# A graph-attention layer that gathers one row per row: own-column rows are gathered again, one table block fewer, x asked for in five requests

## The chip, the core and the metric

The kernel runs on one core of a Trainium2 chip. A core has five engines that run side by side, each with its own stream of instructions: TensorE (PE, matrix products), VectorE (DVE), ScalarE (ACT), GpSimd (POOL) and SyncE (SP, which only asks for transfers). Sixteen transfer engines move data between HBM and the core's memory (SBUF); SP and POOL put requests into queues of their own for them. The metric is the device time of one execution in microseconds. Three runs of the kernel before took 236.44, 237.49 and 237.79 us, median 237.49.

## What is computed

The reference is a graph-attention layer with a residual and a layer norm (4,096 nodes, 512 features, 4 heads):

```python
ht = (h @ W).reshape(N, N_HEADS, N_HIDDEN).transpose(1, 0, 2)
e = leaky_relu(src[:, :, None] + dst[:, None, :], 0.01) + adj_mat[None]
att = softmax(e, axis=-1)
h_prime = einsum('hij,hjd->hid', att, ht).mean(axis=0)
x = layernorm(x + h_prime)
```

adj (4,096 x 4,096, 67 MB) has, on its edges, weights that are uniform from 0.05 to 1e9, and 0 elsewhere; every node has an edge to itself. Against such numbers the scores from `src` and `dst` are tiny. So the softmax of a row is one-hot: all weight lies on the column of the row's largest adj. The kernel uses that: for each row it finds the column of the largest adj, gathers that row of x, multiplies it by the mean of the four heads' W, adds the row's own x and normalises. A test at the end shows whether the largest value led by enough in every row; where not, a general path (the function `general`) computes those blocks in full. With these inputs it is not entered.

## The kernel before, in words

The 4,096 rows are worked through as 32 blocks of 128 rows, one row to a partition. Block 0 is rows 0 to 127; blocks 1 to 31 interleave the others (partition p of block b holds row 128 + 31 p + b - 1). A block of adj is 2 MB; six buffers hold them.

The order of all work is written out by hand (`tc.manual_schedule()`): a loop over steps t = 0 to 31 (lines 536 to 597), and a tail after it (599 to 665). Each engine runs its instructions strictly in the order in which they are written. What happens to a block spreads over steps:

- In step t SP asks for adj of block t + 5 (`load_adj`). Before that, in the steps of the table `x_at` (line 530), it asks for blocks of x into `hold`. All these requests stand in one queue. The two requests for x of eight blocks each are 2 MB, the others in the table 1 MB.
- VectorE reduces adj of block t to maxima of short segments (`segment_maxima`, L208, two halves) and finds the segment that holds the row's maximum (`find_segment`, L215, L217). GpSimd turns that into a row number and fetches the segment itself (`fetch_segment`: `row` L224, `lead` L228).
- Two steps later VectorE finds the column within the segment (`find_column`, L270 and L276), in the steps of `END` (up to 19) behind the step's own `find_segment`, from step 20 on between the two halves of the reduction. GpSimd makes `col` of it (L278) and gathers the rows of x (`gather_rows`).
- At t = block + 3 TensorE turns the gathered rows (`turn`, L290; ScalarE copies the result, L292), adds the row's own x through a product with the identity (`residual`, L302) and multiplies by W (`products`, L309).
- From t = block + 4 on ScalarE takes sums and squares for the layer norm; every fourth step GpSimd makes scale factors of them (`rstd`, L379 to L383), and ScalarE finishes the block (L388) in `hold`, from where it is stored in the tail.

Three ways of gathering exist. In a plain block (0 and 24 to 31) GpSimd gathers all 128 rows (L253). In a block of `TABLED` (1 to 18) the rows whose column is below 128 are not gathered: ScalarE clears the tile one step after the block before (`fill_rows`, L239), GpSimd computes `away` (L245) and `there` (L259), which push such a row's number past the end of x, and gathers with a bounds check (L260), which leaves the cleared row as it is. What is missing is taken from a table of the 128 finished products (`spread`, `from_table`: L337, L339, L341, L349 and `low`, L267). In a block of `OWN` (19 to 23) the rows whose column is their own number are not gathered: ScalarE first copies the block's own x, which is in `hold`, into the tile (L239), and GpSimd computes `away` by comparing with `own` (L247).

GpSimd takes the work of a step in this order: up to step 19 `row`, `lead`, `start` of block t, then column and gather of block t - 2, then `rstd`; from step 20 on column and gather of block t - 2 first, then `row`, `lead`, `start` of block t, then `rstd`. Its requests go into one queue.

Of the kernel before, what the change touches and what calls it, by code (L numbers as in the profile page):

```python
# [9 lines left out]
F32 = mybir.dt.float32  # L10
BF16 = mybir.dt.bfloat16
U32 = mybir.dt.uint32
I32 = mybir.dt.int32
AF = mybir.ActivationFunctionType
OP = mybir.AluOpType
# [6 lines left out]
P = 128  # L22
# [4 lines left out]
EARLY = 18  # L27
LAST = 4
SKIP = 8192
TABLED = range(1, 19)  # L30
OWN = range(19, 24)


@with_exitstack
# [39 lines left out]
def leading_rows(ctx, tc, x, adj, W, a, out, ident, n_bad, any_bad):  # L74
# [8 lines left out]
    nc = tc.nc  # L83
    N, D = x.shape
    H = a.shape[0]
    KB, NB = D // P, N // P
    RB = NB - 1
    AHEAD = 5
    Q = 4
    PIECES = 4  # L90
    LATE = NB - Q
    BEHIND = LATE - Q
# [3 lines left out]
    hold = landing.tile([P, NB, D], F32, name="hold")  # L96
# [5 lines left out]
    once = ctx.enter_context(tc.tile_pool(name="once", bufs=1))  # L102
    small = ctx.enter_context(tc.tile_pool(name="small", bufs=5))
# [18 lines left out]
    def load_adj(ib):  # L122
        if 0 <= ib < NB:
            t = adj_t[ib] = adj_pool.tile([P, N], F32, name="adj_t")
            n = pieces(ib)
            for k in range(n):
                rows_of = adj_rows[ib - 1] if ib else adj[:P, :]
                nc.sync.dma_start(t[:, ts(k, N // n)], rows_of[:, ts(k, N // n)])

    def load_x(lo, n):  # L130
        if lo == 0:
            nc.sync.dma_start(hold[:, 0, :], x[:P, :])
            lo, n = 1, n - 1
        if n:
            nc.sync.dma_start(hold[:, ds(lo, n), :], x_rows[:, ds(lo - 1, n), :])
# [20 lines left out]
    for e, lo, hi in spans:  # L156
        if lo == 0:
            nc.gpsimd.iota(first[:, 0:1], pattern=[[0, 1]], base=0, channel_multiplier=N // e)
            lo = 1
        nc.gpsimd.iota(  # L160
            first[:, lo:hi], pattern=[[N // e, hi - lo]], base=(P + lo - 1) * N // e,
            channel_multiplier=RB * N // e,
# [7 lines left out]
    nc.gpsimd.memset(power, -0.5)  # L170
    eps = once.tile([P, 1], F32, name="eps")
    nc.gpsimd.memset(eps, EPS)
    numbers = once.tile([P, NB], I32, name="numbers")
    nc.gpsimd.iota(numbers, pattern=[[1, NB]], base=P - 1, channel_multiplier=RB)
    own = once.tile([P, NB], F32, name="own")
    nc.gpsimd.tensor_copy(own, numbers)
    zero = once.tile([P, 1], F32, name="zero")
    nc.gpsimd.memset(zero, 0.0)
    nth = once.tile([P, 1], I32, name="nth")
# [19 lines left out]
    low_of, pick_of = {}, {}  # L199

    def segment_maxima(ib, lo, hi):

        e = spans[span_of(ib)][0]
        if lo == 0:
            seg_of[ib] = small.tile([P, N // e], F32, name=f"seg{e}", bufs=2)
        n = max(pieces(ib), 2)
        for k in range(lo * n // PIECES, hi * n // PIECES):
            nc.vector.tensor_reduce(  # L208
                seg_of[ib][:, ts(k, N // e // n)],
                adj_t[ib][:, ts(k, N // n)].rearrange("p (s e) -> p s e", e=e), axis=AX.X, op=OP.max,  # L210
            )

    def find_segment(ib):
        seg = seg_of.pop(ib)
        nc.vector.max(out=top[:, ib, :], in_=seg)  # L215
        at = at_of[ib] = small.tile([P, 8], U32, name="at")
        nc.vector.max_index(at, top[:, ib, :], seg)  # L217
        if ib < NB - 1:
            fetch_segment(ib)
# [14 lines left out]
            start = at_of[ib] = small.tile([P, 1], U32, name="start")  # L234
            nc.gpsimd.tensor_tensor(start, at[:, 0:1], width[:, k : k + 1], op=OP.mult)

    def fill_rows(ib):
        y = y_t[ib] = y_pool.tile([P, D], F32, name="y")
        nc.scalar.copy(y, zero.to_broadcast([P, D]) if ib in TABLED else hold[:, ib, :])  # L239

    def skipped(ib, col):

        away = small.tile([P, 1], U32, name="away")
        if ib in TABLED:
            nc.gpsimd.tensor_scalar(away, col, float(P), float(SKIP), op0=OP.is_lt, op1=OP.mult)  # L245
        else:
            nc.gpsimd.tensor_scalar(away, col, own[:, ib : ib + 1], float(SKIP), op0=OP.is_equal, op1=OP.mult)  # L247
        return away

    def gather_rows(ib, col):  # L250
        if ib not in TABLED and ib not in OWN:
            y = y_t[ib] = y_pool.tile([P, D], F32, name="y")
            nc.gpsimd.indirect_dma_start(  # L253
                out=y, out_offset=None, in_=x,
                in_offset=bass.IndirectOffsetOnAxis(ap=col[:, :1], axis=0),
            )
            return
        there = small.tile([P, 1], U32, name="there")
        nc.gpsimd.tensor_tensor(there, col, skipped(ib, col), op=OP.add)  # L259
        nc.gpsimd.indirect_dma_start(  # L260
            out=y_t[ib], out_offset=None, in_=x,
            in_offset=bass.IndirectOffsetOnAxis(ap=there[:, :1], axis=0),
            bounds_check=N - 1, oob_is_err=False,
        )
        if ib in TABLED:
            low = low_of[ib] = small.tile([P, 1], BF16, name="low")
            nc.gpsimd.tensor_scalar(low, col, float(P), None, op0=OP.min)  # L267

    def find_inner(ib):
        nc.vector.max(out=inner[:, ib, :], in_=lead_of[ib])  # L270
# [1 line left out]
    def find_column(ib):  # L272
        if ib < BEHIND:
            find_inner(ib)
        within = small.tile([P, 8], U32, name="within")
        nc.vector.max_index(within, top[:, ib, :], lead_of[ib])  # L276
        col = small.tile([P, 1], U32, name="col")
        nc.gpsimd.tensor_tensor(col, at_of.pop(ib), within[:, 0:1], op=OP.add)  # L278
        gather_rows(ib, col)
# [71 lines left out]
    def row_norm(ib):  # L351
        sq = rows.tile([P, D], F32, name="sq")
        nc.scalar.activation(sq, hold[:, ib, :], AF.Square, accum_out=xx[:, ib : ib + 1])  # L353
# [24 lines left out]
    def rstd(i):  # L378
        nc.gpsimd.tensor_scalar(sd[:, i], sd[:, i], 1.0 / D, EPS, op0=OP.mult, op1=OP.add)  # L379
        nc.gpsimd.tensor_tensor(sd[:, i], sd[:, i], power[:, : i.stop - i.start], op=OP.pow)  # L380
        nc.gpsimd.tensor_mul(nm[:, i], nm[:, i], sd[:, i])
        if i.stop <= BEHIND:
            nc.gpsimd.tensor_scalar(sd[:, i], sd[:, i], -float(D), None, op0=OP.mult)  # L383
# [61 lines left out]
    def mean_of_heads(kb):  # L445
        o = psum.tile([P, D], F32, name="o")
        for h in range(H):
            nc.tensor.matmul(o, ident, hold[:, w_at + kb * H + h, :], start=(h == 0), stop=(h == H - 1))  # L448
        nc.scalar.activation(w_sum[:, kb, :], o, AF.Copy, scale=1.0 / H)  # L449
# [9 lines left out]
    def square_sums_of_a():  # L459
        sq = rows.tile([P, D], F32, name="sq")  # L460
        nc.scalar.activation(sq[: 2 * H, :], a_rows, AF.Square, accum_out=aa)
# [65 lines left out]
        nc.vector.tensor_reduce(total, pg, axis=AX.X, op=OP.add)  # L527
        nc.vector.tensor_scalar(any_bad, total, -1.0, float(N), op0=OP.mult, op1=OP.add)

    x_at = {Q - 1: (Q, 2 * Q), 3 * Q - 1: (3 * Q, Q), 4 * Q - 1: (4 * Q, 2 * Q)}  # L530
    squares = list(range(KB * H))
    squares_at = {t: 2 if t < 7 else 1 for t in range(3, 15)}
    COLUMN, PROJECT, STATS, FINISH = 2, 3, 4, 8
# [2 lines left out]
    for t in range(NB):  # L536
        if t == NB // 2:
            tc.mark_branch_hint_location("general", engines=HINTED)
        if t in x_at:
            load_x(*x_at[t])  # L540
        if t + AHEAD == NB - 1:
            load_x(LATE, Q)
        load_adj(t + AHEAD)
        middle = 1 if t == NB - 1 else 2
        segment_maxima(t, 0, middle)
        if t >= COLUMN and t not in END and t != COLUMN + 1:
            find_column(t - COLUMN)
        segment_maxima(t, middle, PIECES)
        if t == NB - 1:
            for ib in (BEHIND, BEHIND + 2):  # L550
                load_x(ib, 2)
        find_segment(t)
        if t in END:
            find_column(t - 1 if t <= COLUMN else t - COLUMN)
        if t + 1 in TABLED or t + 1 in OWN:
            fill_rows(t + 1)
        if t >= FINISH and t % Q == 0:
            rstd(slice(t - FINISH, t - FINISH + Q))
        if t < 2:
            mean_of_heads(t)  # L560
        elif t == 2:
            mean_of_heads(2)
            mean_of_heads(3)
            fill_table()
        if t == 0:
            square_sums_of_a()
        if t in (24, 26, 28):
            head_norms((t - 24) // 2)
        ib = t - PROJECT
        if t == NB - 1:  # L570
            for late in range(LATE, NB):
                row_norm(late)
        if t == NB - 2:
            residual(LATE)
            residual(LATE + 1)
        if ib >= 0:
            if ib in TABLED:
                spread(ib)
            turn(ib)
            if ib > BEHIND:  # L580
                products(ib - 1, KB - 1, KB)
            if ib < BEHIND:
                residual(ib)
            if ib in TABLED:
                from_table(ib)
            products(ib, 0, KB if ib < BEHIND else KB - 1)
            if ib == 0:
                split_table()
        for _ in range(squares_at.get(t, 0)):
            square_sum_of_w(squares.pop(0))  # L590
        if t >= BEHIND + STATS:
            put_by(t - STATS)
        elif t >= STATS:
            row_norm(t - STATS)
            parked_stats(t - STATS)
        if t > FINISH:
            finish(t - FINISH - 1)
# [248 lines left out]
```

## Time and profile before

| | |
|---|---|
| median of three runs (lowest, highest) | 237.49 us (236.44, 237.79) |
| profiled execution | 237.14 us |
| its span, first to last instruction | 235.6 us |
| busy: PE, DVE, ACT, POOL | 194.4, 190.9, 143.4, 117.0 us |
| moved | 96.31 MB, mean 409 GB/s |

The span is the profiled part of an execution; 1.54 us lie outside it. The digits of the page's lines are tenths of busy time in 40 slices of the span, 5.9 us each. In a line of the timeline stand the start, the duration, the engine, the line of the program, the operation, output<-input and, in brackets, how long the engine had been idle before and what ended that. A transfer's time to landing runs from its issue to the moment at which its data is there. A window's row ends with the clock that TensorE was granted (1.00 is full), the busy share of the transfer engines, and GB/s.

### The profile page before, as it was taken

How to read it: one execution, taken by the hardware profiler on the slowest of the kernel's cores; microseconds unless marked ns; L12 is line 12 of the kernel's file. 1: busy time of each engine (PE TensorE's matmuls, PEld its weight loads, DVE VectorE, ACT ScalarE, POOL GpSimd, SP SyncE). 2: the span in 40 equal slices, each digit the busy share in tenths (PEclk: the TensorE clock that was granted, in tenths of full speed). 3: DMA queues.
4: the chain of work that ended last, by engine and by line, in shares of the span. 5: the costliest groups of instructions: out<-in, count | busy, mean ns of one | idle time of the engine just before them, and what ended most of it. 6: DMA issues, size and time to landing. Idle time of an engine off the chain costs nothing.

```text
span 235.6 us, 2436 instructions
## 1 busy us (share of the span) xinstructions
PE 194.4 (83%) x573; PEld 92.9 (39%) x580; DVE 190.9 (81%) x301; ACT 143.4 (61%) x348; POOL 117.0 (50%) x275
## 2 busy tenths in 40 slices
PE   0069988778199929999899999999999969999890
PEld 0034443333144424455355444444444424444360
DVE  0538389799829999999999919996999999978782
ACT  3002213678077717899878878887756854399661
POOL 4020425615552775547764765673666447547300
PEclk9999999999679967999999999999999999999999
DMA  6999999999999999999999999999999999999954
GB/s 226 430 428 435 427 428 422 435 436 412 437 423 429 433 426 424 434 419 437 422 431 417 434 429 426 421 430 427 427 432 416 426 423 413 419 424 421 381 204 186
DMA packets 12546, 96.31 MB, mean 409 GB/s; under 512 B 2058, under 2 KB 2506, under 8 KB 7024
## 3 DMA queue, kind: packets, MB, share of 16 engines
q1 hardware_dynamic: 8928, 88.08, 88.5%
q0 software_dynamic: 3584, 8.02, 8.7%
q8 instruction: 5, 0.08, 0.1%
q14 instruction: 13, 0.11, 0.1%
q10 hardware_dynamic: 16, 0.02, 0.0%
HBM read 88.54 MB, written 8.39 MB: 411 GB/s over the span
## 4 chain that ended last, share of the span: by engine, by line
DMA 37%; PE 28%; DVE 10%; POOL 9%; issue 7%; ACT 6%; SPq 0%; POOLq 0%; DVEq 0%
DMA y<-in_x_dram,there 18%; PE o L309 16%; DMA adj_t<-in_adj_dram 14%; DVE seg L208 6%; DMA lead<-in_adj_dram,row 5%; PE o L302 4%; PE tp L290 4%; PE o L349 3%; POOL lead L228 3%; POOL sd L380 2%; PE o L397 2%; ACT yt L292 1%; ACT sq L457 1%; ACT sq L353 1%; DVE col L284 1%
## 5 line engine op out<-in xcount | busy, mean ns | idle before, releaser
L208 DVE TENSOR_REDUCE seg<-adj_t 128x128 f32<-128x2048 f32 (+3 forms) x66 | 144.0, 2209 | 29.1 <-DMA adj_t<-in_adj_dram 29.0
L309 PE MATMUL o<-w_sum,yt 128*128 128x512 f32 x248 | 113.4, 598 | 2.0 <-ACT yt L292 1.9
L309 PEld LDWEIGHTS o<-w_sum,yt 128*128 128x128 f32 x248 | 45.9, 191 | 53.8 <-issue 42.1
L292 ACT COPY yt<-tp 128x512 f32<-128x512 f32 x33 | 19.1, 578 | 33.7 <-PE tp L290 33.6
L228 POOL DMA_INDIRECT lead<-in_adj_dram,row x32 | 32.7, 1023 | 12.4 <-POOL row L224 12.4
L290 PE MATMUL tp<-ident,y 128*128 128x128 f32 x128 | 23.0, 304 | 17.9 <-DMA y<-in_x_dram,there 15.4
L260 POOL DMA_INDIRECT y<-in_x_dram,there x23 | 25.6, 1115 | 15.1 <-POOL there L259 6.8
L290 PEld LDWEIGHTS tp<-ident,y 128*128 128x128 f32 x128 | 18.7, 209 | 32.3 <-issue 30.8
L224 POOL TENSOR_TENSOR row<-at,first 128x1 uint32<-128x1 uint32 x32 | 6.1, 191 | 48.1 <-DVE at L217 43.7
L302 PE MATMUL o<-hold,ident 128*128 128x512 f32 x52 | 28.2, 629 | 0.0
L448 PE MATMUL o<-hold,ident 128*128 128x512 f32 x32 | 16.9, 694 | 13.7 <-DMA hold<-in_L_gnn_W_dram 13.7
L353 ACT ACTIVATE sq<-hold 128x512 f32<-128x512 f32 x32 | 19.9, 624 | 0.0
L388 ACT ACTIVATE hold<-hold,nm,sd 128x512 f32<-128x512 f32 x24 | 19.1, 802 | 0.0
L376 ACT ACTIVATE sq<-hold,nm 128x512 f32<-128x512 f32 x24 | 17.4, 724 | 0.8
L449 ACT ACTIVATE w_sum<-o 128x512 f32<-128x512 f32 x4 | 2.4, 597 | 22.7 <-PE o L448 22.7
L448 PEld LDWEIGHTS o<-hold,ident 128*128 128x128 f32 x32 | 7.1, 225 | 22.7 <-issue 22.2
L339 ACT ACTIVATE off<-px,minus 128x128 f32<-128x128 f32 x18 | 6.6, 368 | 13.9 <-PE px L337 13.9
L374 ACT ACTIVATE hold<-o 128x512 f32<-128x512 f32 x24 | 14.3, 597 | 0.8
L349 PE MATMUL o<-z,pick 128*128 128x512 bf16 x48 | 14.2, 399 | 0.4 <-ACT sq L353 0.2
L215 DVE MAX8 top<-seg 128x8 f32<-128x256 f32 (+2 forms) x32 | 11.6, 361 | 1.1
L217 DVE FIND_INDEX8 at<-top,seg 128x8 uint32<-128x256 f32 (+2 forms) x32 | 11.3, 352 | 0.0
L349 PEld LDWEIGHTS <-pick 128*128 128x128 bf16 x54 | 5.6, 104 | 14.0 <-issue 7.6
(117 smaller groups left out, 190.6 us busy)
## 6 DMA issues: line engine op xcount, KB each, us to landing
adj_t<-in_adj_dram SPq DMA_DIRECT2D x28, 2048.0 KB, 32.5
adj_t<-in_adj_dram SPq DMA_DIRECT2D x6, 1024.0 KB, 24.0
hold<-in_L_gnn_W_dram SPq DMA_DIRECT2D x2, 2048.0 KB, 16.5
hold<-in_x_dram SPq DMA_DIRECT2D x2, 2048.0 KB, 33.6
out_dram<-hold SPq DMA_DIRECT2D x7, 512.0 KB, 4.6
out_dram<-hold SPq DMA_DIRECT2D x3, 1024.0 KB, 13.2
hold<-in_x_dram SPq DMA_DIRECT2D x2, 1024.0 KB, 27.2
adj_t<-in_adj_dram SPq DMA_DIRECT2D x4, 512.0 KB, 19.9
```

Of the source, the lines that this page charges most:

```text
L208: nc.vector.tensor_reduce(seg_of[ib][:, ts(k, N // e // n)], adj_t[ib][:, ts(k, N // n)].rearrange("p (s e) -> p s e", e=e), axis=AX.X, op ...
L228: nc.gpsimd.indirect_dma_start(out=lead, out_offset=None, in_=adj_segs[e], in_offset=bass.IndirectOffsetOnAxis(ap=row[:, :1], axis=0),)
L260: nc.gpsimd.indirect_dma_start(out=y_t[ib], out_offset=None, in_=x, in_offset=bass.IndirectOffsetOnAxis(ap=there[:, :1], axis=0), bounds_c ...
L290: nc.tensor.transpose(tp[:, kb, :], y[:, ds(kb, P, KB)], ident)
L292: nc.scalar.copy(yt, tp)
L302: nc.tensor.matmul(o_ps[ib], ident, hold[:, ib, :], start=start, stop=False)
L309: nc.tensor.matmul(o_ps[ib], yt_of[ib][:, kb, :], w_sum[:, kb, :], start=(start and kb == 0), stop=(kb == KB - 1),)
L349: nc.tensor.matmul(o_ps[ib], pick, z[k], start=(start and k == 0), stop=False)
L353: nc.scalar.activation(sq, hold[:, ib, :], AF.Square, accum_out=xx[:, ib : ib + 1])
L376: nc.scalar.activation(sq, hold[:, ib, :], AF.Square, bias=nm[:, i], scale=-float(D), accum_out=sd[:, i])
L388: nc.scalar.activation(hold[:, ib, :], o, AF.Identity, bias=nm[:, i], scale=sd[:, i])
L448: nc.tensor.matmul(o, ident, hold[:, w_at + kb * H + h, :], start=(h == 0), stop=(h == H - 1))
```

## The change

`OWN` and all that serves it are gone (`own`, `numbers`, the copy of the block's own x, the comparison): blocks 19 to 23 are gathered whole, as plain blocks. Block 18 leaves `TABLED` and becomes a plain block too. `fill_rows` is now `clear_rows` and only clears. The table `x_at` becomes five requests for four blocks of x each, at steps 3 (blocks 4 to 7), 7 (8 to 11), 11 (12 to 15), 15 (16 to 19) and 18 (20 to 23), in place of blocks 4 to 11 at step 3, 12 to 15 at step 11 and 16 to 23 at step 15.

```diff
-TABLED = range(1, 19)
-OWN = range(19, 24)
+TABLED = range(1, 18)
...
-    numbers = once.tile([P, NB], I32, name="numbers")
-    nc.gpsimd.iota(numbers, pattern=[[1, NB]], base=P - 1, channel_multiplier=RB)
-    own = once.tile([P, NB], F32, name="own")
-    nc.gpsimd.tensor_copy(own, numbers)
...
-    def fill_rows(ib):
+    def clear_rows(ib):
         y = y_t[ib] = y_pool.tile([P, D], F32, name="y")
-        nc.scalar.copy(y, zero.to_broadcast([P, D]) if ib in TABLED else hold[:, ib, :])
-
-    def skipped(ib, col):
-
-        away = small.tile([P, 1], U32, name="away")
-        if ib in TABLED:
-            nc.gpsimd.tensor_scalar(away, col, float(P), float(SKIP), op0=OP.is_lt, op1=OP.mult)
-        else:
-            nc.gpsimd.tensor_scalar(away, col, own[:, ib : ib + 1], float(SKIP), op0=OP.is_equal, op1=OP.mult)
-        return away
+        nc.scalar.copy(y, zero.to_broadcast([P, D]))
 
     def gather_rows(ib, col):
-        if ib not in TABLED and ib not in OWN:
+        if ib not in TABLED:
             y = y_t[ib] = y_pool.tile([P, D], F32, name="y")
             nc.gpsimd.indirect_dma_start(
                 out=y, out_offset=None, in_=x,
                 in_offset=bass.IndirectOffsetOnAxis(ap=col[:, :1], axis=0),
             )
             return
+        away = small.tile([P, 1], U32, name="away")
+        nc.gpsimd.tensor_scalar(away, col, float(P), float(SKIP), op0=OP.is_lt, op1=OP.mult)
...
-    x_at = {Q - 1: (Q, 2 * Q), 3 * Q - 1: (3 * Q, Q), 4 * Q - 1: (4 * Q, 2 * Q)}
+    x_at = {lo - 1 - lo // (5 * Q): (lo, Q) for lo in range(Q, BEHIND, Q)}
...
-        if t + 1 in TABLED or t + 1 in OWN:
-            fill_rows(t + 1)
+        if t + 1 in TABLED:
+            clear_rows(t + 1)
```

(Q is 4, BEHIND is 24.) Two places show how the order on the engines moves. The first is SP's queue from the request for adj of block 5 on; a row is one request or several of a kind, 128x4096 of adj is one block, 128x4096 of x eight blocks. Before:

```order
L128 DMA adj_t<-in_adj_dram 128x4096 x3
L135 DMA hold<-in_x_dram 128x4096
L128 DMA adj_t<-in_adj_dram 128x4096 x8
L135 DMA hold<-in_x_dram 128x2048
L128 DMA adj_t<-in_adj_dram 128x4096 x4
L135 DMA hold<-in_x_dram 128x4096
L128 DMA adj_t<-in_adj_dram 128x4096 x8
```

and with the change:

```order
L127 DMA adj_t<-in_adj_dram 128x4096 x3
L134 DMA hold<-in_x_dram 128x2048
L127 DMA adj_t<-in_adj_dram 128x4096 x4
L134 DMA hold<-in_x_dram 128x2048
L127 DMA adj_t<-in_adj_dram 128x4096 x4
L134 DMA hold<-in_x_dram 128x2048
L127 DMA adj_t<-in_adj_dram 128x4096 x4
L134 DMA hold<-in_x_dram 128x2048
L127 DMA adj_t<-in_adj_dram 128x4096 x3
L134 DMA hold<-in_x_dram 128x2048
L127 DMA adj_t<-in_adj_dram 128x4096 x5
```

Half of each large request for x moves back, one half by four blocks of adj (behind the requests for blocks 8 to 11), the other by three (behind those for blocks 20 to 22).

The second place is GpSimd from the `rstd` of step 20 on: the scale factors of blocks 12 to 15, then column and gather of block 19, then `row` and `lead` of block 21 (step 21). Before:

```order
L379 TENSOR_SCALAR sd<-sd 128x4
L380 TENSOR_TENSOR sd<-sd,power 128x4
L381 TENSOR_TENSOR nm<-nm,sd 128x4
L383 TENSOR_SCALAR sd<-sd 128x4
L278 TENSOR_TENSOR col<-start,within 128x1
L247 TENSOR_SCALAR away<-col,own 128x1
L259 TENSOR_TENSOR there<-col,away 128x1
L260 DMA y<-in_x_dram,there 128x512
L224 TENSOR_TENSOR row<-at,first 128x1
L228 DMA lead_1364<-in_adj_dram,row 128x32
```

and with the change:

```order
L366 TENSOR_SCALAR sd<-sd 128x4
L367 TENSOR_TENSOR sd<-sd,power 128x4
L368 TENSOR_TENSOR nm<-nm,sd 128x4
L370 TENSOR_SCALAR sd<-sd 128x4
L265 TENSOR_TENSOR col<-start,within 128x1
L239 DMA y<-in_x_dram,col 128x512
L219 TENSOR_TENSOR row<-at,first 128x1
L223 DMA lead_1342<-in_adj_dram,row 128x32
```

Between column and gather nothing is left; the requests keep their order. The same holds for blocks 18 and 20 to 23.

More of the change, by code (lines that the diff above doesn't have):

```diff
@@ L257, in gather_rows @@
             return
+        away = small.tile([P, 1], U32, name="away")
+        nc.gpsimd.tensor_scalar(away, col, float(P), float(SKIP), op0=OP.is_lt, op1=OP.mult)
         there = small.tile([P, 1], U32, name="there")
-        nc.gpsimd.tensor_tensor(there, col, skipped(ib, col), op=OP.add)
+        nc.gpsimd.tensor_tensor(there, col, away, op=OP.add)
         nc.gpsimd.indirect_dma_start(
@@ L264, in gather_rows @@
         )
-        if ib in TABLED:
-            low = low_of[ib] = small.tile([P, 1], BF16, name="low")
-            nc.gpsimd.tensor_scalar(low, col, float(P), None, op0=OP.min)
+        low = low_of[ib] = small.tile([P, 1], BF16, name="low")
+        nc.gpsimd.tensor_scalar(low, col, float(P), None, op0=OP.min)
     def find_inner(ib):
```

## The prediction

> **What bounds the kernel now.** I read the page first, then who waited for whom on VectorE (DVE), then its timeline, then GpSimd's (POOL). The page:
>
> ```profile
> span 235.6 us, 2436 instructions
> DMA  6999999999999999999999999999999999999954
> q0 software_dynamic: 3584, 8.02, 8.7%
> L260 POOL DMA_INDIRECT y<-in_x_dram,there x23 | 25.6, 1115 | 15.1 <-POOL there L259 6.8 <-ACT y L239 1.4 <-PE px L337 1.3
> ```
>
> The transfer engines are full until about 220 us, so bytes count. But full transfer engines need not mean that the last block of adj is waited for. DVE, which must read every block, tells which it is:
>
> ```profile
> DVE seg L208 <- DMA adj_t<-in_adj_dram: 29.0, 9, 8.7
> DVE inner L270 <- DMA lead<-in_adj_dram,row: 3.5, 4, 1.8
> 68.98 4.48 DVE L208 TENSOR_REDUCE seg<-adj_t 128x128 f32<-128x2048 f32 x2 [4.89 <-DMA adj_t<-in_adj_dram]
> 141.53 2.29 DVE L208 TENSOR_REDUCE seg<-adj_t 128x64 f32<-128x2048 f32 x1 [5.07 <-DMA adj_t<-in_adj_dram]
> 158.59 2.27 DVE L208 TENSOR_REDUCE seg<-adj_t 128x64 f32<-128x2048 f32 x1
> 162.69 0.20 DVE L270 MAX8 inner<-lead 128x8 f32<-128x32 f32 x1 [1.82 <-DMA lead<-in_adj_dram,row]
> 174.16 0.20 DVE L270 MAX8 inner<-lead 128x8 f32<-128x32 f32 x1 [0.55 <-DMA lead<-in_adj_dram,row]
> 183.18 2.27 DVE L208 TENSOR_REDUCE seg<-adj_t 128x64 f32<-128x2048 f32 x1
> ```
>
> The two long waits come at blocks 8 and 20, just behind the two requests for eight blocks of x (2 MB each). After block 20 DVE hardly waits for adj again; between its starts on block 23 (158.59) and block 27 (183.18) it loses 1.82 + 0.55 = 2.37 us to segments (`lead`) that GpSimd fetched late. Was the data there? The requests for blocks 22 and 27, issue and time to landing:
>
> ```profile
> L128 SPq DMA_DIRECT2D adj_t<-in_adj_dram x1: 328/328/328, 118.8 to 118.8; - x1
> DMA to landing us min/median/max: 33.9/33.9/33.9
> ...
> L128 SPq DMA_DIRECT2D adj_t<-in_adj_dram x1: 328/328/328, 151.8 to 151.8; - x1
> DMA to landing us min/median/max: 28.0/28.0/28.0
> ```
>
> Block 22 landed at 152.7, block 27 at 179.8. DVE began block 27 at 183.18, 3.4 us after it was there. That lateness is what can be won; beyond it the arrival of data bounds. The end of the chain hangs on DVE's last blocks:
>
> ```profile
> 205.27 5.88 DMA lead<-in_adj_dram,row
> 213.81 6.42 DMA lead<-in_adj_dram,row
> 226.07 3.55 PE o L397 x16
> ```
>
> The segment of block 30 is fetched after DVE has reduced that block, that of block 31 after it; then come the test, the last products, and the end. Earlier DVE means an earlier end, if TensorE and GpSimd follow.
>
> **The change part by part.**
>
> *More rows gathered.* Block 18 loses its table and blocks 19 to 23 their skipping. Counted from the reference's inputs, 20 rows of block 18 point below column 128, and 48 rows of blocks 19 to 23 at themselves: 68 rows of 2 KB, 0.139 MB. The rate is in this window (GB/s last):
>
> ```profile
> 100.00:110.00 10.00, 9.95 (x34) 5.06 (x34) 9.73 (x16) 9.26 (x25) 5.72 (x13) 1.00 1.01 426
> 104.60:107.40 2.80, 2.75 (x12) 1.40 (x12) 2.80 (x2) 2.43 (x7) 2.33 (x5) 1.00 1.07 447
> ```
>
> 0.139 MB / 426 GB/s = 0.33 us later for everything behind, 0.2 us of it (41 rows, blocks 18 to 20) by block 23. Bounds: 0 where hidden; 0.5 us if these blocks skip as many rows as the average block (8.02 MB in q0, against 8.39 MB of whole gathers and 0.44 MB of segments, leaves 0.81 MB skipped in 23 blocks: 35 KB each, times six).
>
> *x in five requests.* 1 MB takes 1.05/0.426 = 2.46 us. So adj 8 to 11 and 20 to 22 land 2.46 us sooner, and from block 23 on the order of bytes is the old one. SP only gains two more requests; none has a new wait, as the W rows that lay in slots 16 to 23 are long read. What is late next: adj 23, which now stands behind x of blocks 20 to 23. It has no row of its own, but between block 22 (152.7) and block 27 (179.8) lie five steps of 5.4 us, so it lands at 158.1, with the extra rows 158.3. DVE, which starts block 20 2.46 us sooner, is ready before that, and starts block 23 at 158.3 instead of 158.59: **gain 0.3 us** (between 0 and 0.9). The other 2.2 us of the earlier block 20 are waited away there.
>
> *GpSimd's short path.* For blocks 18 to 23 `away` and `there` vanish. The old path in step 21, and the plain path as block 24 has it:
>
> ```profile
> 149.68 0.19 POOL L379 TENSOR_SCALAR sd<-sd 128x4 f32<-128x4 f32 x1 [0.63 <-ACT sq L376]
> 151.59 0.19 POOL L278 TENSOR_TENSOR col<-start,within 128x1 uint32<-128x1 uint32 x1
> 153.10 1.17 POOL L260 DMA_INDIRECT y<-in_x_dram,there  x1 [0.63 <-POOL there L259]
> 154.77 0.97 POOL L228 DMA_INDIRECT lead<-in_adj_dram,row  x1 [0.27 <-POOL row L224]
> ...
> 180.03 0.19 POOL L278 TENSOR_TENSOR col<-start,within 128x1 uint32<-128x1 uint32 x1 [0.36 <-DVE within L276]
> 180.76 0.96 POOL L253 DMA_INDIRECT y<-in_x_dram,col  x1 [0.55 <-POOL col L278]
> ```
>
> From column to gather 1.51 us there, 0.73 us here: 0.78 us less, and the gather itself is 0.15 to 0.2 us shorter. The request for `lead` of block 21 stands behind the gather of block 19 on GpSimd, and lands after it. It landed at 162.69. Now everything ahead of it is sooner: 0.78 us, and up to 2.46 us since DVE found column 19 that much earlier and the statistics that the row at 149.68 waited for follow TensorE, whose blocks from 6 on start from the earlier adj 8. That puts it at 159.5, while DVE asks at 158.3 + 2.3 = 160.6: the 1.82 us vanish. If the statistics came no sooner, 161.9, and 1.3 of the 1.82 us would stay. The 0.55 us of block 23 are less than the 0.78 saved. Against this I leave 0.3 us for later segments, as one lands only some 0.5 us before it is needed: **gain 2.1 us** (between 1.05 and 2.37).
>
> Does a plain gather also land faster? The page's medians say so, the row of block 0 doesn't:
>
> ```profile
> y<-in_x_dram,there POOLq DMA_INDIRECT x23, 8.4
> y<-in_x_dram,col POOLq DMA_INDIRECT x9, 7.1
> ...
> L253 POOL DMA_INDIRECT y<-in_x_dram,col x1: 959/959/959, 26.0 to 26.0; - x1
> DMA to landing us min/median/max: 8.2/8.2/8.2
> ```
>
> Eight of the nine plain gathers run after 180 us, beside the half-wide pieces of the last adj blocks; the ninth took 8.2. I take no gain. (With the medians, 1.3 us more, no segment would be late and the gain in this part 2.37.)
>
> *ScalarE and TensorE.* Five copies and a clearing (0.6 us each), one `off` and one `pick` leave ScalarE, which is 61% busy: nothing. Block 18's table costs TensorE the difference between its block and block 19:
>
> ```profile
> 157.08 0.70 PE L290 MATMUL tp<-ident,y 128*128 128x128 f32 x4
> 162.56 0.63 PE L290 MATMUL tp<-ident,y 128*128 128x128 f32 x4
> 167.40 0.63 PE L290 MATMUL tp<-ident,y 128*128 128x128 f32 x4
> ...
> 194.29 0.72 PE L290 MATMUL tp<-ident,y 128*128 128x128 f32 x4 [1.59 <-DMA y<-in_x_dram,col]
> ```
>
> 5.48 against 4.84, so 0.64 us. TensorE already waits for rows at block 25 (194.29): it is not the bound there, and I count this as cover, not as gain. If it were not there, 0.64 us of the gain would be at risk.
>
> *Sum.* 0.3 + 2.1 = 2.4 us, inside the cap (3.4 - 0.33 = 3.05: data has landed no sooner). The span becomes 233.2; the profiled execution lasted 237.14, 1.54 outside the span, so 234.7 on its terms. The median of the runs shown, 237.49, is 0.35 above that execution. I predict **234.8 us**; own range of this case 234.1 (cap) to 236.1 (1.05 and no more).
>
> **A rule against the change.** While 1 MB of x passed (104.6 to 107.4) the rate was 447 GB/s, no lower than around it. The Trainium skill, "DMA: Bandwidth & Descriptors", section "Bandwidth", has 1 MB moving at 341 GB/s and 16 MB at 425, and asks for large transfers. By it the five requests would take about 0.6 us each more, 3 us in all, and the result would be no faster than before. The trace does not agree: with requests queued behind one another the size does not show.
>
> **The rivals.**
>
> 1. *The segments stay late.* For: GpSimd also does `rstd` every fourth step and a segment queues behind a gather of 8.4 us, which the change leaves. Against: 0.78 us in each of five steps. Then only 0.3 and 0.5 us or so come: 237.14 - 0.8 = 236.3, up to 236.9.
> 2. *The end is held elsewhere* (the stores, ScalarE's row norms before the test). For: the transfer engines are full until 220. Against: the chain has no store in it before the last. Nothing gained, the extra rows paid: 237.14 + 0.33 = 237.5.
> 3. *Slower: TensorE's clock.* TensorE becomes lighter and waits longer for rows, and after long waits it runs at half clock (the clock stands before the DMA share):
>
> ```profile
> 86.86 1.10 PE L290 MATMUL tp<-ident,y 128*128 128x128 f32 x4 [4.59 <-DMA y<-in_x_dram,there]
> 84.00:86.00 2.00, 0.00 (x0) 0.60 1.06 453
> 86.00:90.00 4.00, 2.92 (x7) 0.50 0.98 417
> 94.47 0.70 PE L290 MATMUL tp<-ident,y 128*128 128x128 f32 x4
> ```
>
>    That block took 94.47 - 86.86 = 7.6 us instead of 5.5: 2.1 us. Two such drops in blocks 27 to 31, where nothing is left to make them up, would cost 4.2 and leave 237.14 - 2.4 + 4.2 = 238.9. It decides from waits of somewhat over 2 us there (the clock fell some 2 us into this one); the 1.59 us wait did nothing, and I expect about 1.2. The Trainium skill, "TensorE: Matmul & The Clock Gate", section "Part 1: The HAM clock gate", has the clock fall after an idle window of about 3.4 us. By that the point lies higher and this case is less likely; the trace shows the fall earlier than that.
> 4. *Smaller requests pass slower.* If 1 MB requests made all of x's 5.2 MB take over 3.05 us more (5.24 MB in 12.3 + 3.05 us, a rate under 342 GB/s instead of 426), the data-bound end would be later than now: 237.7 and more. The row at 447 speaks against.
>
> **How the numbers follow.** Forecast 0.60, rival 1 0.22, rival 2 0.09, rival 3 0.06, rival 4 0.03. Half a percent, 1.2 us, is about what a measurement of this kernel can tell from no change; faster means below 236.3. The forecast lies wholly there, with the edge of rival 1: 0.62 faster. The rest of rivals 1 and 2: 0.30 the same. Rivals 3 and 4: 0.08 slower. The range takes in the forecast, rival 1 and most of rival 2: 233.8 to 237.5.
>
> **What would show it.** DVE's wait for adj at blocks 8 and 20 halved (about 2.4 us each), a new one of about 2 us at block 23; no wait of over half a microsecond for `lead` from step 20 on; DVE's start on block 27 at 180 to 181. Column to gather 0.73 us in steps 20 to 25. TensorE's half-clock stretch near 85 us gone or shorter. It is wrong if DVE starts block 27 early and the end does not move (rival 2), or if waits for `lead` of a microsecond remain (rival 1).

## The result: 2 to 3 us faster, with DVE waiting for data in place of segments

The changed kernel took 234.5 us (median; 234.29 to 234.75) against 237.37 us of the kernel before: a ratio of 0.9885, 95% interval 0.9854 to 0.9916. Timed again beside experiments 6 to 8 (below) it took 234.75 against 236.85, ratio 0.9922 [0.9898, 0.9946]. So 2.1 to 2.9 us were won; the forecast was 234.8 us, a gain of 2.4. The profiled execution took 234.5 us, its span is 233.0, which is 2.6 less than before.

The page of the changed kernel: span, the transfer engines by slice, the gathers' queue, and the chain that ended last by engine and by line.

```profile
span 233.0 us, 2399 instructions
DMA  6999999999999999999999999999999999999985
q0 software_dynamic: 3584, 8.16, 8.9%
DMA 64%; DVE 19%; PE 6%; ACT 4%; issue 3%; POOL 1%; SPq 0%; DVEq 0%; POOLq 0%
DMA adj_t<-in_adj_dram 56%; DVE seg L203 16%; DMA hold<-in_L_gnn_W_dram 5%; PE o L296 4%; DMA y<-in_x_dram,col 3%; ACT sq L340 2%; PE o L384 2%; DVE at L212 1%; ACT hold L375 1%; DVE top L210 1%; PE tp L277 1%; DVE within L263 1%; POOL sd L
```

The same two lines of the page before:

```profile
DMA 37%; PE 28%; DVE 10%; POOL 9%; issue 7%; ACT 6%; SPq 0%; POOLq 0%; DVEq 0%
DMA y<-in_x_dram,there 18%; PE o L309 16%; DMA adj_t<-in_adj_dram 14%; DVE seg L208 6%; DMA lead<-in_adj_dram,row 5%; PE o L302 4%; PE tp L290 4%; PE o L349 3%; POOL lead L228 3%; POOL sd L380 2%; PE o L397 2%; ACT yt L292 1%; ACT sq L457 1
```

The chain has changed its kind. Before, it ran through gathers, TensorE, GpSimd and segments; now 56% of it is the arrival of adj and 16% its reduction. GpSimd has fallen from 9% to 1%. A chain is weak evidence by itself, because it follows whichever of several nearly equal waits ended last: that of experiment 3, which won only 0.5 us, also has 44% in the arrival of adj. The waits below say more. The bytes did grow, by 0.14 MB in q0 (the gathers' queue), as worked out.

What DVE waited for, after (us in total, times, longest):

```profile
DVE seg L203 <- DMA adj_t<-in_adj_dram: 29.7, 14, 8.8
DVE within L263 <- DMA lead<-in_adj_dram,row: 0.9, 2, 0.7
```

No wait of `inner` (DVE's first operation on a segment) is left; before there were 4, of 3.5 us in all. The waits for adj add up to the same 29 us in 14 pieces instead of 9. DVE's timeline after, its starts on blocks 8, 12, 16, 20, 23, 26 and 27:

```profile
66.32 4.48 DVE L203 TENSOR_REDUCE seg<-adj_t 128x128 f32<-128x2048 f32 x2 [2.19 <-DMA adj_t<-in_adj_dram]
90.31 4.48 DVE L203 TENSOR_REDUCE seg<-adj_t 128x128 f32<-128x2048 f32 x2 [1.24 <-DMA adj_t<-in_adj_dram]
114.22 4.48 DVE L203 TENSOR_REDUCE seg<-adj_t 128x128 f32<-128x2048 f32 x2 [1.17 <-DMA adj_t<-in_adj_dram]
138.78 2.29 DVE L203 TENSOR_REDUCE seg<-adj_t 128x64 f32<-128x2048 f32 x1 [2.35 <-DMA adj_t<-in_adj_dram]
158.72 2.29 DVE L203 TENSOR_REDUCE seg<-adj_t 128x64 f32<-128x2048 f32 x1 [2.71 <-DMA adj_t<-in_adj_dram]
175.47 2.29 DVE L203 TENSOR_REDUCE seg<-adj_t 128x64 f32<-128x2048 f32 x1 [0.20 <-DMA adj_t<-in_adj_dram]
181.16 2.28 DVE L203 TENSOR_REDUCE seg<-adj_t 128x64 f32<-128x2048 f32 x1
```

Block 23 begins at 158.72, no sooner than before (158.59). Block 27 begins at 181.16, 2.02 us sooner. All the difference on DVE arises between these two, where segments used to be late. The 0.20 us at block 26 shows that DVE has caught up with the data there.

GpSimd's timeline after, the same instructions of step 21 that the prediction quoted of before:

```profile
147.44 0.19 POOL L366 TENSOR_SCALAR sd<-sd 128x4 f32<-128x4 f32 x1 [1.22 <-ACT sq L363]
149.87 1.09 POOL L239 DMA_INDIRECT y<-in_x_dram,col  x1 [0.33 <-POOL col L265]
151.46 0.96 POOL L223 DMA_INDIRECT lead<-in_adj_dram,row  x1 [0.27 <-POOL row L219]
```

The request for block 21's segment left at 151.46 instead of 154.77, and landed 7.4 us later, at 158.9. DVE asked for it at about 161: no wait.

The end of the chain after: one request for adj, the gather behind the last statistics, the last products.

```profile
143.55 31.90 DMA adj_t<-in_adj_dram
196.59 6.92 DMA y<-in_x_dram,col
223.73 3.55 PE o L384 x16
```

The last products start 2.34 us sooner than before (226.07).

### The profile page after: what moved, and what is told of

Its sections match the earlier page's. It is cut to its first block, busy times and chain, and to the rows that moved or that the text cites. A ratio compares the mean times of both kernels' runs of the same rounds, so it can differ in the third digit from the quotient of the medians.

```text
span 233.0 us, 2399 instructions
## 1 busy us (share of the span) xinstructions
PE 194.3 (83%) x570; PEld 92.6 (40%) x576; DVE 191.1 (82%) x301; ACT 139.8 (60%) x340; POOL 112.9 (48%) x260
## 4 chain that ended last, share of the span: by engine, by line
DMA 64%; DVE 19%; PE 6%; ACT 4%; issue 3%; POOL 1%; SPq 0%; DVEq 0%; POOLq 0%
DMA adj_t<-in_adj_dram 56%; DVE seg L203 16%; DMA hold<-in_L_gnn_W_dram 5%; PE o L296 4%; DMA y<-in_x_dram,col 3%; ACT sq L340 2%; PE o L384 2%; DVE at L212 1%; ACT hold L375 1%; DVE top L210 1%; PE tp L277 1%; DVE within L263 1%; POOL sd L367 0%; POOL lead L223 0%; ACT yt L279 0%
## 5 line engine op out<-in xcount | busy, mean ns | idle before, releaser
L277 PE MATMUL tp<-ident,y 128*128 128x128 f32 x128 | 22.5, 300 | 15.9 <-DMA y<-in_x_dram,there 12.0
L435 PE MATMUL o<-hold,ident 128*128 128x512 f32 x32 | 17.0, 699 | 13.7 <-DMA hold<-in_L_gnn_W_dram 13.7
L289 PE MATMUL o<-hold,ident 128*128 128x512 f32 x52 | 27.5, 614 | 0.0
L248 POOL DMA_INDIRECT y<-in_x_dram,there x17 | 18.9, 1111 | 10.9 <-POOL there L247 5.6
L239 POOL DMA_INDIRECT y<-in_x_dram,col x15 | 14.9, 995 | 7.6 <-POOL col L265 7.0
```

The costliest lines, as they stand in the source:

```text
L239: nc.gpsimd.indirect_dma_start(out=y, out_offset=None, in_=x, in_offset=bass.IndirectOffsetOnAxis(ap=col[:, :1], axis=0),)
L248: nc.gpsimd.indirect_dma_start(out=y_t[ib], out_offset=None, in_=x, in_offset=bass.IndirectOffsetOnAxis(ap=there[:, :1], axis=0), bounds_c ...
L277: nc.tensor.transpose(tp[:, kb, :], y[:, ds(kb, P, KB)], ident)
L289: nc.tensor.matmul(o_ps[ib], ident, hold[:, ib, :], start=start, stop=False)
```

## The experiments

Each kernel was timed against the kernel before on its own chip: the first four together (before: median 236.66 us), the next four (236.85), the last four (236.67). Ratios have their 95% interval.

**1. The rows alone.** The changed kernel with the old table of requests:

```diff
-    x_at = {lo - 1 - lo // (5 * Q): (lo, Q) for lo in range(Q, BEHIND, Q)}
+    x_at = {Q - 1: (Q, 2 * Q), 3 * Q - 1: (3 * Q, Q), 4 * Q - 1: (4 * Q, 2 * Q)}
```

> The changed kernel with x asked for as before (eight blocks at step 3, four at 11, eight at 15). My theory, as predicted: the short path on GpSimd for blocks 18 to 23 is the larger part. Block 20 of adj comes at 141.5 again, so only 0.78 us of the 3.3 us by which the segment of block 21 was fetched sooner remain; the wait for it falls from 1.82 to about 1 us, the 0.55 us wait vanishes, DVE starts block 27 at about 182.0 (183.18 before, 181.16 with the whole change), and the time is 1.2 to 1.6 us under the kernel before. Rival, that x's five requests alone are what pays: no gain, within 0.4 us of the kernel before. Rival, that the requests do nothing: the whole 2.7 us.

Measured: 234.69 us, ratio 0.9924 [0.9895, 0.9954]. That is the whole gain, without the requests, and more than the 1.2 to 1.6 us that were expected. The trace caught an execution of 235.78 us, 1.1 above the kernel's median. In it, GpSimd:

```profile
150.31 0.19 POOL L366 TENSOR_SCALAR sd<-sd 128x4 f32<-128x4 f32 x1 [1.44 <-ACT sq L363]
154.34 0.97 POOL L223 DMA_INDIRECT lead<-in_adj_dram,row  x1 [0.27 <-POOL row L219]
```

and DVE at block 21's segment:

```profile
162.34 0.20 DVE L257 MAX8 inner<-lead 128x8 f32<-128x32 f32 x1 [1.07 <-DMA lead<-in_adj_dram,row]
```

Here the statistics came 0.63 us later than before (150.31 against 149.68). That took back more than half of the 1.06 us by which the path from them to the segment's request is shorter (4.03 us against 5.09), and DVE still waits 1.07 us of the 1.82. This is the case that the prediction allowed for ("If the statistics came no sooner"), and it costs about what it said: this execution begins block 27 at 182.10, 1.08 us sooner than before. Four of the six executions took 234.45 to 234.78 us; none of them was traced, so what gave them the last microsecond was not seen.

**2. The requests alone**, with all of the old rows:

```diff
-    x_at = {Q - 1: (Q, 2 * Q), 3 * Q - 1: (3 * Q, Q), 4 * Q - 1: (4 * Q, 2 * Q)}
+    x_at = {lo - 1 - lo // (5 * Q): (lo, Q) for lo in range(Q, BEHIND, Q)}
```

> The kernel before with x asked for as in the change, own-column rows kept. Theory: the copy of x of block 20 that ScalarE makes in step 19 (at about 144 us before) must now wait for x of blocks 20 to 23, which lands behind adj 22, at about 152.5. ScalarE takes its work in order, so TensorE, the statistics and GpSimd's rstd of step 20 stand behind it for 7 to 9 us, the segment of block 21 comes as late, and DVE waits for it: time 3 to 7 us over the kernel before. Rival, that five requests are good by themselves: 1 to 2.5 us under it.

Measured: 243.77 us, ratio 1.0293 [1.0269, 1.0316], 7.1 us slower. ScalarE, then GpSimd, then DVE:

```profile
153.23 0.62 ACT L239 COPY y<-hold 128x512 f32<-128x512 f32 x1 [10.56 <-DMA hold<-in_x_dram]
```

```profile
157.21 0.19 POOL L379 TENSOR_SCALAR sd<-sd 128x4 f32<-128x4 f32 x1 [10.36 <-ACT sq L376]
162.29 0.96 POOL L228 DMA_INDIRECT lead<-in_adj_dram,row  x1 [0.27 <-POOL row L224]
```

```profile
170.37 0.20 DVE L270 MAX8 inner<-lead 128x8 f32<-128x32 f32 x1 [10.07 <-DMA lead<-in_adj_dram,row]
```

The copy of block 20's own x waits 10.6 us for x that was asked for at step 18. Behind it on ScalarE stand the statistics, behind these on GpSimd the segment, and DVE waits 10.1 us. So the two parts of the change are not independent: the late request is only possible because the own-row copies are gone.

**3. The requests, early enough for the own rows.** The kernel before with five requests, the last at step 16:

```diff
+    x_at = {3: (4, 4), 7: (8, 4), 11: (12, 4), 15: (16, 4), 16: (20, 4)}
```

> The kernel before with x asked for in five requests, the last at step 16 and not 18, so that the copies of own rows find it in time. GpSimd's path stays long. Adj 8 to 11 and 20 come 2.46 us sooner, adj 21 and later as before. If the short path is what pays: the waits for segments stay near 1.8 and 0.5 us and the time is within 0.5 us of the kernel before. If it is rather that TensorE, and so the statistics that GpSimd waits for in step 20, come sooner from block 6 on: the wait for the segment of block 21 falls to 0.3 us or less, and the time is 1.3 to 1.8 us under the kernel before.

Measured: 236.17 us, ratio 0.9978 [0.9961, 0.9995], 0.5 us faster. DVE's starts on block 21 and on the segment of that block:

```profile
147.87 2.29 DVE L208 TENSOR_REDUCE seg<-adj_t 128x64 f32<-128x2048 f32 x1 [3.15 <-DMA adj_t<-in_adj_dram]
161.50 0.20 DVE L270 MAX8 inner<-lead 128x8 f32<-128x32 f32 x1 [0.51 <-DMA lead<-in_adj_dram,row]
```

What block 20 gains is waited away one block later: block 21 begins 0.83 us later than before (147.04). The segment of block 21 does come 1.2 us sooner (161.50 against 162.69), but it and that of block 23 are still late, by 0.51 and 0.60 us. This lies between the two outcomes that were expected for block 21 (near 1.8 us, or at most 0.3).

**4. Only the first request split** (blocks 4 to 11), in the kernel before:

```diff
+    x_at = {3: (4, 4), 7: (8, 4), 11: (12, 4), 15: (16, 8)}
```

> The kernel before with only the first request for eight blocks of x split (blocks 4 to 7 at step 3, 8 to 11 at step 7); the second stays whole at step 15. DVE starts block 20 at 141.5 as before. If TensorE's earlier start in blocks 6 and on is what frees GpSimd in step 20, rstd runs 2 us sooner there and the wait for the segment of block 21 falls from 1.82 to 0.3 to 0.6 us: time 1.2 to 1.5 us under the kernel before. If only the short path or the later half of x pays: within 0.4 us of the kernel before.

Measured: 236.72 us, ratio 1.0000 [0.9987, 1.0013]. TensorE did start its blocks 2.2 us sooner (block 17 at 149.34 against 151.55), but GpSimd did not use it:

```profile
149.42 0.19 POOL L379 TENSOR_SCALAR sd<-sd 128x4 f32<-128x4 f32 x1
154.51 0.97 POOL L228 DMA_INDIRECT lead<-in_adj_dram,row  x1 [0.27 <-POOL row L224]
```

The row at 149.42 waits for nothing: it stands in GpSimd's order behind the segment request of block 20, which follows DVE's late block 20. In this order a TensorE that is ahead gives GpSimd sooner scale factors only if block 20 comes sooner too. DVE's waits for the segments of blocks 21 and 23 were 0.97 and 0.65 us here.

**5. The changed kernel again**, for the next three.

> The changed kernel itself, on the same chip as the three runs beside it. The whole change: 2.4 to 2.8 us under the kernel before (ratio 0.9885).

Measured: 234.75 us, ratio 0.9922 [0.9898, 0.9946]; block 23 at 158.71, block 27 at 181.15.

**6. The rows alone, with the long path.** As 1, with two operations between column and gather in blocks 18 to 23 that change no value:

```diff
+            if 18 <= ib < BEHIND:
+                none = small.tile([P, 1], U32, name="away")
+                nc.gpsimd.tensor_scalar(none, col, 0.0, float(SKIP), op0=OP.is_lt, op1=OP.mult)
+                same = small.tile([P, 1], U32, name="there")
+                nc.gpsimd.tensor_tensor(same, col, none, op=OP.add)
+                col = same
```

> The changed kernel with x asked for as before, and two operations put back between column and gather on GpSimd in blocks 18 to 23: a comparison that never holds and an addition of its zero. Rows are gathered whole, ScalarE makes no copies and block 18 has no table, as in the change; only GpSimd's path is long again. If the 0.78 us of GpSimd's path are the cause: waits for segments of 1.5 us and more in steps 22 to 25, and at most 0.5 us of the 1.8 us that the rows gained without these operations are left. If the gain came from ScalarE's missing copies, TensorE's missing table or the plain gather: 1.5 us or more under the kernel before, as without them.

Measured: 236.68 us, ratio 0.9992 [0.9974, 1.0011]. The gain of experiment 1 is gone. Two operations of 0.2 us each, which with the gaps around them lengthen GpSimd's path in step 21 by 0.84 us (4.87 against 4.03), on an engine that is half idle, are worth 1.6 us by the ratios and 2.0 by the medians. DVE at block 21's segment and at block 27:

```profile
162.12 0.20 DVE L263 MAX8 inner<-lead 128x8 f32<-128x32 f32 x1 [0.84 <-DMA lead<-in_adj_dram,row]
182.35 2.28 DVE L203 TENSOR_REDUCE seg<-adj_t 128x64 f32<-128x2048 f32 x1
```

The waits for segments in steps 22, 23 and 25 were 0.69, 0.84 and 0.39 us. The two traces, of 1 and of 6, hardly differ (block 27 at 182.10 and 182.35), because the traced execution of 1 was one of its two longer ones. The difference between 1 and 6 rests on the times: the four short executions of 1 (up to 234.78 us) lie below all twelve of 6 (from 235.39 us).

**7. The whole change, with the long path.** The same lines in the changed kernel.

> The whole change with the same two operations put back. In the trace of the change the segments of blocks 21 and 22 landed 2 us and more before they were asked for, those of blocks 23 and 24 0.4 to 0.6 us before. Theory: 0.78 us more in each step therefore costs only 0.2 to 0.6 us in all, the five requests having given the slack (DVE waits for adj 23 meanwhile). If the short path is worth the same with and without the requests: 1.5 us and more over the changed kernel.

Measured: 234.71 us, ratio 0.993 [0.9905, 0.9954], no different from 5. GpSimd and DVE:

```profile
148.15 0.19 POOL L372 TENSOR_SCALAR sd<-sd 128x4 f32<-128x4 f32 x1 [1.64 <-ACT sq L369]
153.02 0.96 POOL L223 DMA_INDIRECT lead<-in_adj_dram,row  x1 [0.27 <-POOL row L219]
```

```profile
161.01 0.20 DVE L263 MAX8 inner<-lead 128x8 f32<-128x32 f32 x1 [0.25 <-DMA lead<-in_adj_dram,row]
181.46 2.28 DVE L203 TENSOR_REDUCE seg<-adj_t 128x64 f32<-128x2048 f32 x1
```

With the requests, block 20 and the statistics come sooner, and that alone brings the segment to within 0.25 us of its need. So 1, 6 and 7 together say: **with whole rows, short path and requests are substitutes**. Either gives the gain; both together give it once, since then the data bounds. For the requests a trace shows how (7); for the short path alone only the times do.

**8. Statistics behind the column** in steps 24 and 28, a trial at a faster version. The 1.9 us of `rstd` stand ahead of a gather on the chain above (196.59):

```diff
+            if t in (24, 28):
+                rstd(slice(t - FINISH, t - FINISH + Q))
...
-        if t >= FINISH and t % Q == 0:
+        if t >= FINISH and t % Q == 0 and t not in (24, 28):
```

The added lines stand between `find_column` and `find_segment`.

> The changed kernel with rstd of steps 24 and 28 moved on GpSimd: behind the gather and ahead of the row and segment of the step, instead of behind them. In the trace of the change rstd of step 28 (1.9 us) holds up the gather of block 27 by some 1.3 us, and the chain that ended last runs through that gather to ScalarE's row norms. Ahead of the row GpSimd waits 1.15 us for DVE anyway. Theory: the gather of block 27 issues 1.2 to 1.5 us sooner, the segment of block 28 0.7 us later but in time, and the time falls by 0.2 to 0.8 us against the changed kernel. Rival: the end hangs on the segment of block 31 alone, then within 0.2 us of the changed kernel.

Measured: 234.56 us, ratio 0.9915 [0.9895, 0.9936], not distinguishable from 5. A miss: the gather did leave 1.2 us sooner (195.38 against 196.59) and the last products started 0.65 us sooner:

```profile
223.08 3.55 PE o L384 x16
```

but the span is 232.9, only 0.1 less. The last store took 0.5 us more from its issue to the end of the span (228.7 to 232.9, against 229.3 to 233.0).

**9. x of blocks 24 to 27 at step 20** instead of step 31, in the changed kernel: 1 MB put ahead of the last blocks of adj, with nothing else moved.

```diff
+        if t == 20:
+            load_x(BEHIND, Q)
...
-        if t == NB - 1:
-            for ib in (BEHIND, BEHIND + 2):
-                load_x(ib, 2)
```

> The changed kernel with x of blocks 24 to 27 (1 MB) asked for at step 20 and not at step 31: adj 25 to 31 land 2.46 us later, the bytes are the same. In the trace of the change DVE waits for adj of block 26, so it has no lateness in hand there. Theory, that data now bounds DVE to block 26: DVE starts block 27 about 2.2 us later and the time rises by 1.2 to 2.4 us against the changed kernel. Rival, that GpSimd's path still sets the pace: within 0.4 us of it.

Measured: 237.19 us, ratio 1.0009 [0.9986, 1.0033]. DVE's starts on blocks 25 and 27:

```profile
172.37 2.29 DVE L203 TENSOR_REDUCE seg<-adj_t 128x64 f32<-128x2048 f32 x1 [2.54 <-DMA adj_t<-in_adj_dram]
183.49 2.27 DVE L203 TENSOR_REDUCE seg<-adj_t 128x64 f32<-128x2048 f32 x1
```

1 MB at the 426 GB/s of the prediction's window is 2.46 us; DVE waited 2.54 us for adj at block 25 and the whole gain went. The changed kernel has no lateness in hand at this place.

**10. The same in the kernel before.**

> The same move in the kernel before. There DVE came to block 26 at 177.4 and to block 27 at 183.2, while adj lands at 174.3 and 179.8. 2.46 us later it would land at 176.8 and 182.3, still ahead of DVE. Theory: the time stays within 0.5 us of the kernel before. Rival, that data bounded the kernel before too: 1.2 to 2.4 us over it.

Measured: 237.06 us, ratio 1.0023 [1.0008, 1.0038]. The same megabyte costs 0.4 us here. DVE's starts on blocks 25 and 27:

```profile
171.76 2.29 DVE L208 TENSOR_REDUCE seg<-adj_t 128x64 f32<-128x2048 f32 x1 [0.96 <-DMA adj_t<-in_adj_dram]
182.93 2.27 DVE L208 TENSOR_REDUCE seg<-adj_t 128x64 f32<-128x2048 f32 x1
```

The pair 9 and 10 measures what the prediction's first part claimed: DVE in the kernel before was behind its data, by about 2 us (2.46 less the 0.4 that it cost), and in the changed one it is not. The 3.4 us that the prediction read at block 27 of one trace are more than this.

**11. Block 18 keeps its table** (`TABLED = range(1, 19)`), else as changed.

> The whole change except that block 18 keeps its table (20 rows fewer gathered, GpSimd's long path in step 20, one table product more on TensorE). In the trace of the change the segment of block 20 lands at 151.6 and is asked for at 153, so 0.8 us more there is hidden, as are TensorE's 0.64 us. Theory: within 0.3 us of the changed kernel. Rival, that block 18's part counts: 0.5 us or more over it.

Measured: 234.4 us, ratio 0.9902 [0.9884, 0.992], block 23 at 158.64. This edit of the change makes no difference that can be told from 5.

**12. A quarter of the output not stored.** The changed kernel without the stores of blocks 0 to 7, so 2 MB less pass in the tail (the output lacks the rows of blocks 0 to 7):

```diff
-    for ib in range(0, 2 * Q, Q):
-        store(nc.sync, ib, Q)
```

> The changed kernel without the stores of blocks 0 to 7: the output lacks their rows, all else is computed. 2 MB, 4.9 us of the transfer engines, leave the tail; everything up to the landing of adj 31 is as it was. If the end of the changed kernel is bounded by transfers (late stores queue behind early ones, and the last gathers beside them): 0.5 to 1.5 us under the changed kernel. If the chain of engines alone sets the end: within 0.3 us of it.

Measured: 234.5 us, ratio 0.9899 [0.9877, 0.992], span 233.0. A window of the tail, transfer share and GB/s last:

```profile
220.00:224.00 4.00, 4.00 (x14) 2.05 (x13) 3.50 (x9) 2.04 (x5) 1.28 (x3) 1.00 1.00 417
```

in the changed kernel, and without those stores

```profile
220.00:224.00 4.00, 4.00 (x14) 1.96 (x13) 3.46 (x10) 2.03 (x5) 1.27 (x3) 1.00 0.22 90
```

The transfer engines fell to 22% busy and the end did not move: the full slices of the tail bound nothing.

**From block 27 to the end.** The traces give DVE's start on block 27 and the span:

| kernel | block 27 | span | between |
|---|---|---|---|
| before | 183.18 | 235.6 | 52.4 |
| changed | 181.16 | 233.0 | 51.8 |
| 1, rows alone | 182.10 | 234.2 | 52.1 |
| 2, requests alone | 190.13 | 242.3 | 52.2 |
| 6, rows alone, long path | 182.35 | 234.6 | 52.3 |
| 7, whole, long path | 181.46 | 232.9 | 51.4 |
| 9, x early, changed | 183.49 | 235.6 | 52.1 |
| 10, x early, before | 182.93 | 234.9 | 52.0 |

While block 27 moves by 9 us, the rest stays within 51.4 to 52.4 us; the traces of 3, 4, 5, 8, 11 and 12 give 51.7 to 52.3. The prediction's step "earlier DVE means an earlier end" holds from both sides.

## Why the prediction was right

**The bound.** Right, and shown by 9 and 10: DVE behind its data before, level with it after. Its size was less than the 3.4 us read, about 2 us.

**Segments, the 2.1 us.** Right in size: from block 23 to block 27 DVE took 183.18 - 158.59 = 24.59 us before and 181.16 - 158.72 = 22.44 after, 2.15 less. Part of that may be scatter of the one trace of before: in the traces of 4 and 10, whose rows are the old ones, the same stretch takes 23.74 and 23.90. Block 21's segment landed at 158.9 where 159.5 was forecast. Its request moved 3.31 us, 2.24 of it from the statistics (149.68 to 147.44) and 1.07 from the path behind them (column to gather took 0.52 us, where 0.73 was forecast and 1.51 stood before). The prediction took these as adding up. At the request they do, in the time they don't: 1 and 7 show that either is enough. Its reason for the sooner statistics, TensorE's earlier blocks, was half of it; by 4, block 20 must come sooner as well.

**Requests, the 0.3 us.** This term failed. Block 23 was forecast at 158.3 and began at 158.72 (158.71 again), 0.13 later than before. The forecast interpolated arrivals evenly between blocks 22 and 27. What the requests give instead is the second way to the same gain. The waits were forecast well where they were forecast: about 2.4 at blocks 8 and 20 (2.19 and 2.35), about 2 at block 23 (2.71). Those at blocks 12 and 16 (1.24 and 1.17) were not.

**The sum** came out partly by luck: block 27, forecast at 180 to 181, began at 181.16. What was missing there was made up behind it, 0.6 us less between that block and the end (0.4 in the repeat), where nothing was forecast. DVE's waits for segments behind block 27 also fell, from 1.40 + 0.68 us to 0.70 + 0.24, and the last segment took 5.6 us from issue to landing against 6.42. With the scatter of the table, the runs do not show whether this is the cause.

**Extra rows, 0.33 us.** The bytes are as worked out. Their time was not measured by itself; experiment 11 returns 20 of the 68 rows and moves block 23 by 0.07 us, where 0.1 would follow, but the traces of 7 and 12 differ by more than that from each other (158.48 and 158.74).

**A plain gather is no faster**: right. Those of blocks 18 to 23 took 7.2 to 8.8 us. Only beside the half-wide pieces of the last blocks do they take about 6 to 7 us (6.92 in the row at 196.59).

**The rivals.** 1 fell in the changed kernel: up to block 27 DVE waits for no segment. The sign that no wait would exceed half a microsecond failed once, with 0.70 us in the tail (at 204.29). What rival 1 describes is experiment 6, 236.68 us against its 236.3 to 236.9. 2 fell by the table and by 12. 3 fell for blocks 27 to 31: TensorE's waits for rows there were at most 1.09 us, about as expected, and the clock stayed full until the last products. 4 fell: splitting a 2 MB request cost nothing in experiment 4. The prediction's window of 447 GB/s begins too early, since that x landed at 108.5 (79.5 + 29.0); over 106.0 to 108.5 the rate was 430 GB/s, so its reading holds. The Trainium skill, "DMA: Bandwidth & Descriptors", section "Bandwidth", has 1 MB move at 341 GB/s against 425 at 16 MB, for transfers issued from GpSimd. For SP's requests, which queue behind one another here, the runs show no such loss.

**What stays open.** Why 8 moved TensorE's end by 0.65 us and the span by 0.1 (12 speaks against the volume of stores as the reason; one last store per trace is too few). When the statistics came in the executions of 1 at 234.5 us is open too.

## What to carry to other kernels

Ask of each engine how far it is behind its data, not how busy the transfer engines are: a test like 9 and 10, a known transfer put ahead of the data, measures that lateness directly. Two parts of a change that feed the same wait should not be summed; price each with the other in place and with the other gone. A request moved back must be checked against every engine that reads its data, and against what is queued behind that reader: here 7 us hung on a copy of 0.6.

## What the hardware did unexpectedly

TensorE's clock fell after a wait shorter than the "somewhat over 2 us" that the prediction gave. TensorE in the changed kernel, its start on block 7, and the granted clock (the number before the transfer share):

```profile
90.25 0.72 PE L277 MATMUL tp<-ident,y 128*128 128x128 f32 x4 [1.90 <-DMA y<-in_x_dram,there]
88.00:90.00 2.00, 0.36 (x2) 1.00 1.07 451
90.00:92.00 2.00, 1.75 (x7) 0.89 0.99 420
92.00:95.00 3.00, 3.00 (x6) 0.50 1.00 424
95.00:97.00 2.00, 2.00 (x5) 1.00 0.99 423
```

The half clock came over a microsecond after work had resumed and lasted about 3.4 us (block 7 took 7.25 us instead of 5.5). The stretch of before, from 84.0 to 91.2, is gone, as the prediction expected. In experiment 3 a wait of 1.88 us at the same place did the same. In experiment 9 one of 1.85 us did not:

```profile
90.30 0.72 PE L277 MATMUL tp<-ident,y 128*128 128x128 f32 x4 [1.85 <-DMA y<-in_x_dram,there]
92.00:95.00 3.00, 3.00 (x10) 1.00 1.02 431
```

nor did 1.76 us in experiment 4 or 1.87 us at block 15 in experiment 7. A wait of 2.56 us at block 23 in experiment 9 did (half clock from 184.1 to 187.4); it came after DVE's wait at block 25 (172.37), so that wait has another cause. The waits of 1.85 to 1.90 us lie too close together to give a threshold. The Trainium skill, "TensorE: Matmul & The Clock Gate", section "Part 1: The HAM clock gate", has a free-running window of about 3.4 us and a fall after an idle one. The length of the stretch agrees with that figure; the fall after 1.9 us of idle time doesn't. The fall in the changed kernel cost nothing at the end: the repeat had a wait of 0.87 us and no fall there, and began block 27 at the same time (181.15 against 181.16).
